# Down products of two blocks at a time: their 64-row rests in the two halves of the array's rows, each in its own PSUM bank

## The chip, the cores and the metric

The kernel runs on one core of a Trainium2 chip. The metric is the device time in microseconds of one execution; three runs of the kernel before give 792.35, 794.47 and 799.27 us, with a median of 794.47.

## The reference, cut to what matters

The whole computes two residual layers on 8 x 512 tokens of width 256. The first layer is a LoRA projection and a fake-quantised gated FFN. The second is the one the change touches: a per-language adapter with a norm, a router that takes the best two of nine experts for each token, and a gated FFN of inner width 704 in each expert.

```python
def _L1_ffn_ref(x, Wr, Wg, Wu, Wd):
    logits = jnp.einsum('bsh,he->bse', x, Wr)
    probs = jax.nn.softmax(logits, axis=-1)
    topk_w, topk_idx = jax.lax.top_k(probs, TOP_K)
    topk_w = topk_w / jnp.sum(topk_w, axis=-1, keepdims=True)
...
    gate = jax.nn.silu(jnp.einsum('th,ehi->tei', xf, Wg))
    hidden = gate * jnp.einsum('th,ehi->tei', xf, Wu)
    out = jnp.einsum('tei,eih,te->th', hidden, Wd, cw)
```

All of the second FFN is computed in f32. The inner width is 704 = 5 x 128 + 64: five full chunks of 128 rows and a rest of 64.

## The kernel before, in words

**Stages.** The first layer works with activations laid out with the width over the partitions: `lora_in` and `lora_out` (L258, L273) do the LoRA products in pairs of batches, a pair in the two halves of the array (64 columns each in L262, 64 rows each in L278, where each half writes its own PSUM bank); `gate_chunk` and `last_chunk` the quantised gate and up products. Then a software pipeline over 8 batches (the loop at L907) runs `down_and_add` (L469, bf16, five 128-row products and one 64-row product L477 for each bank), the adapter (L484, L512), transposes (L497, L557), the router (`choose`, L569) and `hand_out` (L603), which scatters each token's row to the list of each of its two experts in DRAM.

**Blocks.** The lists are worked off in blocks of 128 rows, each with one expert's weights; 72 blocks are planned for and 67 are used in the shown inputs. One block is: `fetch_rows`, `fetch_gate_up` and `fetch_down` (L792 to L817) by transfers of SyncE's queue; `turn` (L819), two transposes of the rows and a copy by ScalarE; `gate_up` (L828), 11 chunks of 128 columns by 2 products of 128 rows into three PSUM banks, then silu by ScalarE and the multiplication by VectorE into `hid` (128 x 6 x 128); `down` (L859), six products of `hid` against the down weights into one bank; then VectorE multiplies with the token's weight into `y` (L866) and GpSimd starts an indirect transfer that adds the 128 rows into the output (L867).

**The rest of 64 rows.** The last chunk of the inner width has 64 rows. The down weights hold these 64 rows twice, once in each half of the partitions of chunk 5. `hid[64:128, 5]` gets the rest (L848), and `hid[0:64, 5]` is set to zero once for each of the three `hid` buffers (L929 to L931), so that the sixth product can be a full one of 128 rows (L864).

**Order and buffers.** TensorE's and SyncE's orders are written by hand (`manual_schedule`, L900); those of the other engines are left to a scheduler. For block i TensorE does `gate_up(i)`, `turn(i + 1)`, then `down(i - 1)` (`first_half`, L886, and `second_half`, L893). Ten blocks are woven into the batch loop (`SLOTS`, L905); blocks 10 to 63 follow in the loop at L958, and the rest under a branch for each (L966), which ends with the last `down`. PSUM's eight banks are taken in turn (L447): three for a `gate_up`, one for a `turn`, one for a `down`. There are three buffers each of gate and up weights, down weights, `hid`, `g`, `y` and the token weights, and eight of rows. `ask(rows, gu, dn)` (L879) requests transfers up to the given block: gate and up weights of block i + 3 behind `gate_up(i)`, down weights of block i + 2 behind `down(i - 1)`. A block's weights are transferred only if its expert is not that of the block three before it. Before block 16 SyncE also writes the pad rows of the lists (`write_pads`, L758).

Of the kernel before, what the change touches and what calls it, by code (L numbers as in the profile page):

```python
# [28 lines left out]
ALU = mybir.AluOpType  # L29
AX = mybir.AxisListType  # L30

P = 128
# [6 lines left out]
def adaln_ffn_kernel(  # L39
# [21 lines left out]
    nc = tc.nc  # L61
# [3 lines left out]
    NL1, D, A = W1.shape  # L65
# [7 lines left out]
    NM = (I + P - 1) // P  # L73
# [11 lines left out]
    def act_scale(top, sig, name):  # L85
# [26 lines left out]
    start = rt.tile([P, NJ, E], F32, name="start")  # L112
    nc.gpsimd.iota(
        start, pattern=[[0, NJ], [CAP, E]], base=0, channel_multiplier=0, allow_small_or_imprecise_dtypes=True
# [6 lines left out]
    full = NM - 1  # L121
    last = rows[-1]
# [319 lines left out]
    def in_turn(name, of):  # L442

        turn_of[name] = turn_of.get(name, -1) + 1
        return of[turn_of[name] % len(of)]

    def bank(name):  # L447
        return in_turn("bank", banks_sb)
# [11 lines left out]
    def quantise(b):  # L460
        batches[b]["hq"] = hq = hq_sb[b % 2]
        batches[b]["x"] = x_sb[:, b]
        h = h_full(b // 2)[:, :, b % 2]
        for m0, m1 in ((0, 1), (1, 3), (3, 5)) if b == 0 else ((0, 3), (3, 5)):
            rounded(hq[:, m0:m1], h[:, m0:m1], rh)()
        if b % 2 == 0:
            rounded(hl_sb[b // 2 % 2], h_last(b // 2), rh)()
# [12 lines left out]
    def adapter_in(b):  # L480
        st = batches[b]
        ph = bank("ph")
        for c in range(KC):
            nc.tensor.matmul(  # L484
                ph[:A], lhsT=st["w1"][:, c], rhs=st["x"][:, c], start=c == 0, stop=c == KC - 1
            )
        st["ha"] = ha = ha_sb[b % 2]
        nc.scalar.activation(ha[:A], ph[:A], AF.Relu, bias=st["b1c"])
# [62 lines left out]
    def turn_z(b):  # L551
        st = batches[b]
        st["zT"] = zT = ad.tile([P, KC, S], F32, name="zT")
        for c in range(KC):
            pt = bank("pt3")
            for j in range(NJ):
                nc.tensor.transpose(  # L557
                    pt[:, j * P : (j + 1) * P], st["row"][:, j, c * P : (c + 1) * P], ident
                )
            nc.scalar.copy(zT[:, c], pt)  # L560
# [81 lines left out]
    SURE = 2 * T // P  # L642
    NW = 3
# [121 lines left out]
    AHEAD = 4  # L765
# [3 lines left out]
    def where_h_was(k, n):  # L769
        got = flat_h[k][:, at_[0] : at_[0] + n]  # L770
        at_[0] += n
        return got
# [9 lines left out]
    hid_sb = [where_h_was(1, NM * P).rearrange("p (m t) -> p m t", t=P) for _ in range(3)]  # L782
# [7 lines left out]
    steps = [dict() for _ in range(NBLK)]  # L790
# [28 lines left out]
    def turn(i):  # L819
        st = steps[i]  # L820
        xb = st["xb"]
        pt = bank("pt4")
        for c in range(KC):
            nc.tensor.transpose(pt[:, c * P : (c + 1) * P], xb[:, c * P : (c + 1) * P], ident)  # L824
        st["xbT"] = xbT = in_turn("xbT", xbT_sb)
        nc.scalar.copy(xbT.rearrange("p c t -> p (c t)"), pt[:, :D])  # L826

    def gate_up(i):  # L828
        st = steps[i]

        gu, xbT = st["gu"], st["xbT"]
        pa, pb, pd = bank("pga"), bank("pgb"), bank("pgc")
        spots = [(pa, m * P) for m in range(4)] + [(pb, m * P) for m in range(4)] + [(pd, 0), (pd, P), (pd, 2 * P)]
        st["hid"] = hid = in_turn("hid", hid_sb)
        g = in_turn("g", g_sb)
        for n, (bk, at) in enumerate(spots):
            for c in range(KC):
                nc.tensor.matmul(  # L838
                    bk[:, at : at + P], lhsT=gu[:, c, n * P : (n + 1) * P], rhs=xbT[:, c], start=c == 0, stop=c == KC - 1
                )  # L840
        nc.scalar.activation(g[:, :4].rearrange("p m t -> p (m t)"), pa, AF.Silu)  # L841
        nc.vector.tensor_tensor(  # L842
            hid[:, :4].rearrange("p m t -> p (m t)"), pb, g[:, :4].rearrange("p m t -> p (m t)"), ALU.mult
        )
        nc.scalar.activation(g[:, 4], pd[:, :P], AF.Silu)  # L845
        nc.vector.tensor_tensor(hid[:, 4], pd[:, P : 2 * P], g[:, 4], ALU.mult)  # L846
        nc.scalar.activation(g[last : 2 * last, 5], pd[:last, 2 * P : 3 * P], AF.Silu)  # L847
        nc.vector.tensor_tensor(  # L848
            hid[last : 2 * last, 5], pd[last : 2 * last, 2 * P : 3 * P], g[last : 2 * last, 5], ALU.mult
        )  # L850

        xb = st["xb"]
        m0, dw, wt = (in_turn(n, small_[n]) for n in ("m0", "dw", "wt"))
        nc.vector.tensor_scalar(m0, xb[:, D + 3 : D + 4], expert[:, i : i + 1], None, ALU.is_equal)
        nc.vector.tensor_tensor(dw, xb[:, D + 1 : D + 2], xb[:, D + 2 : D + 3], ALU.subtract)
        nc.vector.scalar_tensor_tensor(wt, dw, m0, xb[:, D + 2 : D + 3], ALU.mult, ALU.add)  # L856
        st["wt"] = wt

    def down(i):  # L859
        st = steps[i]  # L860
        hid, dn = st["hid"], st["dn"]
        po = bank("po")
        for m in range(NM):
            nc.tensor.matmul(po[:, :D], lhsT=hid[:, m], rhs=dn[:, m], start=m == 0, stop=m == NM - 1)  # L864
        y = in_turn("y", y_sb)
        nc.vector.tensor_scalar(y, po[:, :D], st["wt"], None, ALU.mult)  # L866
        nc.gpsimd.indirect_dma_start(  # L867
            out=out,
            out_offset=bass.IndirectOffsetOnAxis(ap=st["xb"][:, D : D + 1].bitcast(I32), axis=0),
            in_=y,  # L870
            in_offset=None,
            compute_op=ALU.add,
        )
# [5 lines left out]
    def ask(rows, gu, dn):  # L879

        for name, fetch, n in (("rows", fetch_rows, rows), ("gu", fetch_gate_up, gu), ("dn", fetch_down, dn)):
            while asked[name] < min(n, asked["planned"]):
                fetch(asked[name])
                asked[name] += 1

    def first_half(i):  # L886

        gate_up(i)
        ask(i + 1 + AHEAD, i + 1 + NW, i + NW - 1)
        if i + 1 < NBLK:  # L890
            turn(i + 1)

    def second_half(i):  # L893

        if i > 0:
            down(i - 1)
            ask(0, 0, i + NW)


    with tc.manual_schedule(engines={mybir.EngineType.SP, mybir.EngineType.PE}):  # L900
        quantise(0)
        quantise(1)
        done = 0

        SLOTS = {5: 1, 6: 2, 7: 2, 8: 2, 9: 1, 10: 2}  # L905
        PLANS = {4: 0, 8: 1, 10: 2}
        for i in range(B + 3):  # L907
            slots = SLOTS.get(i, 0)
            f = PLANS.get(i)
            if 1 <= i <= B:  # L910
                adapter_in(i - 1)
            if slots > 1:
                first_half(done)
            if 1 <= i <= B:
                turn_x(i - 1)
            if 3 <= i:
                hand_out(i - 3)
            if f is not None:
                plan_counts(f)
            if slots > 1:  # L920
                second_half(done)
                done += 1
            if i < B:
                down_and_add(i)
            if f is not None:
                plan_order(f)
            if i + 2 < B:
                quantise(i + 2)
            if i == 3:  # L929
                for hid in hid_sb:  # L930
                    nc.gpsimd.memset(hid[:last, full], 0.0)  # L931
            if 2 <= i < B + 2:
                turn_z(i - 2)
            if slots:
                if done == 0:
                    turn(0)
                first_half(done)
            if 1 <= i <= B:
                adapter_out_and_moments(i - 1)
            if f is not None:  # L940
                plan_blocks(f)
            if slots:
                second_half(done)
                done += 1
            if 1 <= i and i + 1 < B:
                fetch_adapter(i + 1)
            if 2 <= i < B + 2:
                choose(i - 2)
            if 1 <= i <= B:
                norm(i - 1)  # L950
            if f is not None and f < 2:
                asked["planned"] = ENDS[f + 1]
                if f == 0:
                    ask(0, 1, 1)
                    ask(1, 2, 2)
                ask(done + AHEAD, done + NW, done + NW - 1)
        pads_at = done + 6
        for i in range(done, SURE):  # L958
            if i == pads_at:
                write_pads()  # L960
                asked["planned"] = NBLK
            first_half(i)
            second_half(i)
    n_used = nc.values_load(used[0:1, 0:1], min_val=SURE - ENDS[2], max_val=NBLK - ENDS[2])

    def rest(i):  # L966
# [80 lines left out]
```

## Time and profile before

| What | us |
|---|---|
| Runs: lowest, median, highest | 792.35, 794.47, 799.27 |
| Profiled execution: its own time | 789.34 |
| Its span (first to last instruction) | 787.4 |
| TensorE busy, in matmuls | 707.1 (90%) |
| VectorE, ScalarE, GpSimd busy | 314.4, 222.2, 200.9 |
| First `gate_up` (block 0) starts | 201.9 |
| Block 10's `gate_up` starts | 335.9 |
| Last `down` ends on TensorE | 779.4 |

How to read it: the page divides the span into 40 slices of 19.7 us, with one digit for the busy tenths of each engine. A group of instructions is named by its line, engine, operation, and tiles written and read; "128*128 128x256 f32" of a matmul gives the rows and columns of the array that are used and the rows and columns of the moving operand. The end of a matmul in the records is modelled and overlaps the next one, so the distance between two starts tells the cost, not the recorded length. The profiled execution took 2 us more than its span.

### The profile page before, as it was taken

How to read it: one execution, taken by the hardware profiler on the slowest of the kernel's cores; microseconds unless marked ns; L12 is line 12 of the kernel's file. 1: busy time of each engine (PE TensorE's matmuls, PEld its weight loads, DVE VectorE, ACT ScalarE, POOL GpSimd, SP SyncE). 2: the span in 40 equal slices, each digit the busy share in tenths (PEclk: the TensorE clock that was granted, in tenths of full speed). 3: DMA queues.
4: the chain of work that ended last, by engine and by line, in shares of the span. 5: the costliest groups of instructions: out<-in, count | busy, mean ns of one | idle time of the engine just before them, and what ended most of it. 6: DMA issues, size and time to landing. Idle time of an engine off the chain costs nothing. (4 is left out here: it accounts for less than half of the span.)

```text
span 787.4 us, 13732 instructions
## 1 busy us (share of the span) xinstructions
PE 707.1 (90%) x4717; PEld 602.0 (76%) x4728; DVE 314.4 (40%) x1087; ACT 222.2 (28%) x439; POOL 200.9 (26%) x173
## 2 busy tenths in 40 slices
PE   7497596775799976999999999999999999999995
PEld 2233234552687866999999999999999999999995
DVE  3769864554356445422222222222222222222221
ACT  4588583342132132111111111211111111212110
POOL 1045500440323454241212122121212121221212
PEclk9799885666699988999999999999999999999999
DMA  9500011332846847632337331238942468315642
GB/s 344 163 1 2 0 34 48 101 102 81 328 136 168 301 129 266 204 82 35 78 82 236 105 81 29 42 102 275 333 107 40 144 218 266 79 28 156 180 116 30
DMA packets 44522, 103.38 MB, mean 131 GB/s; under 512 B 8216, under 2 KB 33824, under 8 KB 41120
## 3 DMA queue, kind: packets, MB, share of 16 engines
q1 hardware_dynamic: 31584, 85.13, 31.7%
q0 software_dynamic: 12720, 17.31, 12.2%
q8 instruction: 39, 0.64, 0.3%
q14 instruction: 35, 0.29, 0.1%
q10 hardware_dynamic: 144, 0.01, 0.0%
HBM read 176.86 MB, written 22.83 MB: 254 GB/s over the span
## 5 line engine op out<-in xcount | busy, mean ns | idle before, releaser
L838 PEld LDWEIGHTS bank<-upper__107,lower 128*128 128x128 f32 x2948 | 342.8, 194 | 7.1 <-issue 3.2
L838 PE MATMUL bank<-upper__107,lower 128*128 128x128 f32 x2948 | 344.3, 277 | 0.5 <-ACT upper__107 L826 0.5
L864 PE MATMUL bank<-upper__107 128*128 128x256 f32 x528 | 124.1, 385 | 0.0
L842 DVE TENSOR_TENSOR upper__107<-bank,upper__107 128x512 f32<-128x512 f32 x67 | 46.3, 691 | 178.6 <-PE bank L838 178.5
L864 PEld LDWEIGHTS bank<-upper__107 128*128 128x128 f32 x528 | 98.6, 193 | 12.2
L867 POOL DMA_INDIRECT out_dram<-upper__107,lower x35 | 54.8, 1565 | 189.7 <-DVE wt L856 133.8
L841 ACT ACTIVATE upper__107<-bank 128x512 f32<-128x512 f32 x67 | 39.9, 596 | 224.0 <-PE bank L838 224.0
L867 POOL DMA_INDIRECT out_dram<-upper__107 x32 | 50.0, 1564 | 180.7 <-DVE wt L856 154.1
L631 POOL DMA_INDIRECT lists<-row,sloti x64 | 63.0, 984 | 121.5 <-DMA lower<-lists 34.4
L866 DVE TENSOR_SCALAR upper__107<-bank,wt 128x256 f32<-128x256 f32 x67 | 32.4, 484 | 96.9 <-PE bank L864 96.7
L845 ACT ACTIVATE upper__107<-bank 128x128 f32<-128x128 f32 x67 | 18.6, 277 | 162.7 <-PE bank L838 162.7
L864 PE MATMUL bank<-lower,upper__107 128*128 128x256 f32 x276 | 63.5, 380 | 0.4 <-issue 0.4
L864 PEld LDWEIGHTS bank<-lower,upper__107 128*128 128x128 f32 x276 | 50.7, 190 | 6.8 <-issue 0.8
L846 DVE TENSOR_TENSOR upper__107<-bank,upper__107 128x128 f32<-128x128 f32 x67 | 19.5, 291 | 59.2 <-ACT upper__107 L845 59.2
L557 PE MATMUL bank<-ident,row 128*128 128x128 f32 x64 | 13.0, 370 | 21.5 <-DVE row L549 18.4
L848 DVE TENSOR_TENSOR upper__107<-bank,upper__107 64x128 f32<-64x128 f32 x67 | 19.7, 294 | 20.9 <-ACT upper__107 L847 20.3
L557 PEld LDWEIGHTS bank<-ident,row 128*128 128x128 f32 x64 | 10.4, 192 | 22.9 <-issue 18.6
L826 ACT COPY upper__107<-bank 128x256 f32<-128x256 f32 x68 | 25.3, 372 | 9.0 <-PE bank L824 8.8
L375 ACT ACTIVATE g<-pg,swg 128x1024 f32<-128x1024 f32 (+1 forms) x24 | 24.8, 1049 | 9.8 <-PE pg L363 6.6
L379 POOL TENSOR_TENSOR lower<-u,g 128x1024 f32<-128x1024 f32 x6 | 14.1, 2356 | 47.8 <-ACT u L378 47.8
L363 PE MATMUL pg<-yq,wgT 128*128 128x512 bf16 x79 | 22.6, 405 | 4.0 <-DVE yq L163 2.2
L476 PE MATMUL bank<-yq,wdT 128*128 128x512 bf16 x73 | 21.4, 409 | 3.2 <-DVE yq L163 2.5
(203 smaller groups left out, 663.2 us busy)
## 6 DMA issues: line engine op xcount, KB each, us to landing
lower<-in_L_ffn_W_dram SPq DMA_DIRECT2D x70, 1408.0 KB
upper__107<-in_L_ffn_W_dram SPq DMA_DIRECT2D x46, 768.0 KB
lower<-in_L_ffn_W_dram SPq DMA_DIRECT2D x23, 768.0 KB
lower<-lists SPq DMA_DIRECT2D x36, 130.0 KB
upper__107<-lists SPq DMA_DIRECT2D x35, 130.0 KB
x_sb<-in_x_dram SPq DMA_DIRECT2D x8, 512.0 KB
out_dram<-xtok SPq DMA_DIRECT2D x8, 512.0 KB
lists<-pad SPq DMA_DIRECT2D x10, 130.0 KB
```

The costliest lines, as they stand in the source:

```text
L363: nc.tensor.matmul(p[:, z * S : (z + 1) * S], lhsT=w[:, c, ms], rhs=yq[:, 2 * k + z, c], start=c == 0, stop=c == KC - 1,)
L375: nc.scalar.activation(g, pg[:, :n], AF.Silu, scale=swg[:, m : m + 1])
L476: nc.tensor.matmul(pd, lhsT=wdT[:, m, cs], rhs=hq[:, m], start=m == 0, stop=False)
L557: nc.tensor.transpose(pt[:, j * P : (j + 1) * P], st["row"][:, j, c * P : (c + 1) * P], ident)
L631: nc.gpsimd.indirect_dma_start(out=own_rows[(b * NJ + j) * 2 + k], out_offset=bass.IndirectOffsetOnAxis(ap=sloti[:, j, k : k + 1], axis=0) ...
L826: nc.scalar.copy(xbT.rearrange("p c t -> p (c t)"), pt[:, :D])
L838: nc.tensor.matmul(bk[:, at : at + P], lhsT=gu[:, c, n * P : (n + 1) * P], rhs=xbT[:, c], start=c == 0, stop=c == KC - 1)
L841: nc.scalar.activation(g[:, :4].rearrange("p m t -> p (m t)"), pa, AF.Silu)
L842: nc.vector.tensor_tensor(hid[:, :4].rearrange("p m t -> p (m t)"), pb, g[:, :4].rearrange("p m t -> p (m t)"), ALU.mult)
L864: nc.tensor.matmul(po[:, :D], lhsT=hid[:, m], rhs=dn[:, m], start=m == 0, stop=m == NM - 1)
L866: nc.vector.tensor_scalar(y, po[:, :D], st["wt"], None, ALU.mult)
L867: nc.gpsimd.indirect_dma_start(out=out, out_offset=bass.IndirectOffsetOnAxis(ap=st["xb"][:, D : D + 1].bitcast(I32), axis=0), in_=y, in_of ...
```

## The change

From block 10 on, blocks go by twos: `gate_up(i)`, `turn(i + 1)`, `gate_up(i + 1)`, `turn(i + 2)`, then the downs of blocks i - 1 and i together: five 128-row products of the one into its bank, five of the other into its bank, then the two 64-row rests behind each other. A block of odd number keeps its rest in partitions 0 to 63 of `hid`'s chunk 5, one of even number in 64 to 127 (`half`), so the two rests of a pair lie in different halves of the array's rows. The zeroing of the unused half is gone. The blocks woven into the batch loop, and those under the branches, still do one down at a time, its last product now over 64 rows. Down weights of two blocks are requested behind each pair.

```diff
+    def half(i):
+        return slice(0, last) if i % 2 else slice(last, 2 * last)
...
-            hid[last : 2 * last, 5], pd[last : 2 * last, 2 * P : 3 * P], g[last : 2 * last, 5], ALU.mult
+            hid[half(i), full], pd[last : 2 * last, 2 * P : 3 * P], g[last : 2 * last, 5], ALU.mult
...
-    def down(i):
+    def down(*blocks):
+
+        for i in blocks:
+            st = steps[i]
+            st["po"] = po = bank("po")
+            for m in range(full):
+                nc.tensor.matmul(po[:, :D], lhsT=st["hid"][:, m], rhs=st["dn"][:, m], start=m == 0, stop=False)
+        for i in blocks:
+            st = steps[i]
+            hs = half(i)
+            nc.tensor.matmul(st["po"][:, :D], lhsT=st["hid"][hs, full], rhs=st["dn"][hs, full], start=False, stop=True)
+        for i in blocks:
+            weigh_and_add(i)
+
+    def weigh_and_add(i):
         st = steps[i]
-        hid, dn = st["hid"], st["dn"]
-        po = bank("po")
-        for m in range(NM):
-            nc.tensor.matmul(po[:, :D], lhsT=hid[:, m], rhs=dn[:, m], start=m == 0, stop=m == NM - 1)
+        po = st["po"]
         y = in_turn("y", y_sb)
         nc.vector.tensor_scalar(y, po[:, :D], st["wt"], None, ALU.mult)
         nc.gpsimd.indirect_dma_start(
...
-    def first_half(i):
+    def first_half(i, downs_left=1):
 
         gate_up(i)
-        ask(i + 1 + AHEAD, i + 1 + NW, i + NW - 1)
+        ask(i + 1 + AHEAD, i + 1 + NW, i + NW - downs_left)
...
-            if i == 3:
-                for hid in hid_sb:
-                    nc.gpsimd.memset(hid[:last, full], 0.0)
...
-        for i in range(done, SURE):
+        assert (SURE - done) % 2 == 0 and pads_at % 2 == done % 2
+        for i in range(done, SURE, 2):
             if i == pads_at:
                 write_pads()
                 asked["planned"] = NBLK
             first_half(i)
-            second_half(i)
+            first_half(i + 1, 2)
+            down(i - 1, i)
+            ask(0, 0, i + 1 + NW)
```

## The prediction, made before the changed kernel ran

> **What bounds the kernel now.** I read the page first (busy shares and slices), then who waited for whom on TensorE over the block loop, then TensorE's timeline in the loop and in the early stages where the array already works on parts of its rows or columns.
>
> ```profile
> PE 707.1 (90%) x4717; PEld 602.0 (76%) x4728; DVE 314.4 (40%) x1087; ACT 222.2 (28%) x439; POOL 200.9 (26%) x173
> PE   7497596775799976999999999999999999999995
> PEclk9799885666699988999999999999999999999999
> L838 PE MATMUL bank<-upper__107,lower 128*128 128x128 f32 x2948 | 344.3, 277 | 0.5 <-ACT upper__107 L826 0.5
> L864 PE MATMUL bank<-upper__107 128*128 128x256 f32 x528 | 124.1, 385 | 0.0
> ```
> TensorE is at 9 in every slice from 335 us on, at a granted clock of 9 and more. 2948 is 67 x 44: a block's 22 gate and up products (11 chunks by 2) each leave two records, two passes of an f32 product; the down products too (528 + 276 = 67 x 12, for 6).
>
> The waits of TensorE between 330 and 780 us have one row in all:
> ```profile
> PE bank L864 <- issue: 0.4, 1, 0.4
> ```
> So from 330 us to the end the time is the sum of TensorE's passes. One block in its timeline (start, length, line):
> ```profile
> 335.86 5.07 PE L838 MATMUL bank<-upper__107,lower 128*128 128x128 f32 x44
> 340.77 0.38 PE L824 MATMUL bank<-ident,lower 128*128 128x128 f32 x2
> 340.99 2.76 PE L864 MATMUL bank<-lower,upper__107 128*128 128x256 f32 x12
> 343.58 5.07 PE L838 MATMUL bank<-upper__107,lower 128*128 128x128 f32 x44
> ```
> From start to start: 44 passes in 4.91 us, 12 down passes in 2.59 us (0.216 us each), a block in 7.72 us. The 379 ns of a record overlap the next; the pace is what costs.
>
> [...] The LoRA stage at the start has the very form of the change, 64-row f32 products in both row halves into two banks (L278, four products of 512 columns a time):
> ```profile
> 14.00 1.99 PE L278 MATMUL py<-t,small_sb 64*128 64x512 f32 x8
> 15.92 1.94 PE L262 MATMUL pr<-x_sb,small_sb 128*64 128x512 f32 x8
> 17.79 1.99 PE L278 MATMUL py<-t,small_sb 64*128 64x512 f32 x8
> ```
> Eight passes of 512 columns at the loop's pace are 8 x 0.432 = 3.46 us one after another; the eight took 1.92 us from the first to the next line's first. The single records start in twos, 5 to 7 ns apart. So the halves do run together, also in f32: 4 x 0.432 = 1.73, and 0.19 us is left over per visit. That rest is the change of mode: in the single records the first L278 starts 521 ns after the last L262 where 429 is the pace (0.092, the drain), and the next 534 ns later (0.105, the load of 128 columns). Two other places agree:
> ```profile
> 227.10 1.25 PE L476 MATMUL bank<-yq,wdT 128*128 128x512 bf16 x5
> 228.29 0.39 PE L477 MATMUL bank<-yq,wdT 64*128 64x512 bf16 x1
> 228.61 1.09 PE L557 MATMUL bank<-ident,row 128*128 128x128 f32 x8
> ```
> ```profile
> 240.77 1.93 PE L484 MATMUL bank<-x_sb,w 128*64 128x512 f32 x4
> 242.63 5.18 PE L838 MATMUL bank<-upper__107,lower 128*128 128x128 f32 x44
> 247.64 0.38 PE L824 MATMUL bank<-ident,upper__107 128*128 128x128 f32 x2
> ```
> L477 is a 64-row product behind 128-row ones in one accumulation, as the change makes it. Five L476 take 1.19 us to L477's start instead of 5 x 0.216 = 1.08, and L477 takes 0.32 instead of 0.216: about 0.10 for each of the two drains (bf16 weights, 10 ns of load). L838 behind a 64-column mode takes 5.01 us for its 44 passes instead of 4.91: another 0.10[...]. So one change of mode into f32 products costs about 0.093 drain + 0.105 load = 0.20 us.
>
> **The change part by part.** The program order shows the TensorE rows: two gate_ups, then ten 128-row down products, then the two 64-row ones, 27 times (blocks 9 to 62); blocks 0 to 8 and 63 to 66 keep one down each, now ended by one 64-row product.
>
> *Pairs.* Removed: two sixth products run one after another, 4 passes x 0.216 = 0.864. Added: drain and load 0.093 + 0.105, two overlapped passes 2 x 0.216 = 0.432 and 7 ns of stagger, drain and load of the next gate_up 0.093 + 0.102: 0.832. Gain 0.03 us a pair, 27 x 0.03 = -0.9 us. Bounds: the two mode changes measured between 0.17 and 0.21 each, so 0.01 to 0.09 a pair, -0.3 to -2.4.
>
> *Single downs.* A 64-row product takes as long as a 128-row one (L477 beside L476), so these only pay: 0.39 us where a 128-row f32 product follows, 0.30 where bf16 follows (L476), 0.20 where the next product (9 rows, L719) changed the mode before as well. In the tail, d63 and d64 pay 0.39 each on the full path, d65 only its entry 0.20; d66's scatter waits for d65's at 780.7, with its own y ready at 780.4, so its 0.2 is covered: +1.0 us. Early: d0 0.30, d1 0.39, d2 0.30, d3 0.39, d4 0.35 (it runs at half clock), d5 0.39, d6 0.39, d7 0.20, d8 0.39: 3.1 us. The first four, 1.4 us, stand ahead of a wait of TensorE of 4.85 us (L700 at 280.5 us for VectorE), whose chain goes over scatters that only partly start from TensorE: I count half, 0.7. After it the chain goes through TensorE at each step (the waits of 2.3 and 4.7 us at 299 and 302 us begin at its L569), so d4 to d8, 1.7 us, count but for 0.2 at a wait of 0.35 us: early +2.2, bounds +1.2 and +3.1.
>
> *Moved work.* A down of the first block of a pair comes one gate_up later, so y, its multiplication (484 ns) and its scatter (1.56 us on GpSimd, landing some 4 us later) come two at a time each 15.4 us: VectorE is busy 29% of the loop and GpSimd 20%, cover enough. In VectorE's order both y stand behind the second block's hid, which the next pair needs 10 us later: nothing. The 8 banks turn 10 times a pair, and each bank comes back over 5 us after its reader could start: nothing. The three hid buffers are all in use at a pair, but block i+2 writes behind the pair on TensorE anyway. SyncE asks the down weights of i+2 and i+3 together after the pair; for i+2 the time from request to use falls from 20.5 us (three blocks less a down) to 12.4 (two gate_ups 10.26, five products 2.16). In the trace the packets of such a load end 4.7 to 5.6 us after the request, with six full blocks in a row between 527 and 577 us: 7 us of cover. The requests behind those two in SyncE's order are for gate and up weights of blocks two pairs ahead. The nine pad writes (383 to 392 us) stay ahead of block 16; behind them the request for block 19 comes 5 us before use instead of 8, and no weight packets move there (none between 331 and 411 us). The three memsets left out ended at 123 us, GpSimd then waited 18 us for VectorE: nothing.
>
> *Sum.* -0.9 + 1.0 + 2.2 = +2.3 us on the profiled execution's 789.34 (span 787.4): 791.6. The shown runs have a median of 794.47, 5.1 above it, so 796.8 is my figure for a median.
>
> **The rivals.** (1) The mode change is cheap for f32 here: weights are loaded ahead, only drains are paid. Then a pair gains 0.864 - 0.432 - 0.19 = 0.24, -6.5, singles pay about half, +1.6: 789.6. If even the drain vanished, 27 x 0.43 = -11.6: 783. For it: in L278 loads for the second passes do go ahead within a mode. Against: the 0.10 at L838 and L477, every time. (2) It ends slower: the halves don't overlap, because the two accumulate behind 128-row products of their own banks and follow each other; decided by whether the second product starts 7 ns or 0.43 us after the first. Then a pair loses 0.40, +10.8, singles +3.2: 808.5. Against: L278 starts in twos with two banks. (3) Late weights: if a down load took over 12.4 us from request to landing, TensorE would stand in about 13 pairs with a fresh load; 1 us each gives 810, with 7 us of measured cover against it. (4) The switch is paid, but the early waits hide all: +0.5, 795.
>
> **How the numbers follow.** My case 0.80 (with (4) in its range), its own range 793 to 802: +0.5 to +3.9 and the spread of the shown runs, -2 to +5. Rival (1) 0.08 with drains alone and 0.03 without, (2) 0.05, (3) 0.04. The likeliest is 796.8; 788.5 to 804 takes in the cheap switch and leaves out the free one and both slow ones. One per cent (7.9 us) is about what can be told from no change. Over 1% faster: the free switch and some scatter, 0.06. Over 1% slower: (2), (3), scatter, 0.12. Within: 0.82.
>
> **What would show it.** In the changed profile's loop: the ten down passes of two blocks 20 x 0.216 = 4.3 us, then 64-row passes starting 7 ns apart, the first of them 0.31 after the last 128-row one; from the first 64-row start to the next gate_up 0.63 us; that gate_up's 44 passes 5.01 us; a pair in 15.41 us against 15.45. Passes 0.216 apart in the halves would prove (2), 0.22 ahead of the halves (1), a wait of TensorE for a transfer (3). What would make me wrong: a shift of the stages before 330 us by more than 3 us.

## The result, and the profile after

The changed kernel takes 816.94 us (median of 6 runs, 815.01 to 819.06) beside 794.05 us for the kernel before on the same chip: a ratio of 1.0275, 95% interval 1.0247 to 1.0304. It is slower by 19.6 to 24.1 us, where I had forecast +2.3 us and a range that ended at 804. The profiled execution took 819.02 us with a span of 817.2. That span is 29.8 us longer than the one before, more than the 22.9 us between the medians: the profile before (789.34) lies below all six runs of its kernel here, the profile after at the top of its own. The ratios and intervals of this document are taken over executions at the chip's usual speed (one slow execution of experiment 1 is left out), and are not the quotients of the medians that stand beside them.

On the page, TensorE is busier in microseconds and less busy as a share:
```profile
PE 719.7 (88%) x4717; PEld 588.3 (72%) x4728; DVE 308.1 (38%) x1087; ACT 221.8 (27%) x439; POOL 201.3 (25%) x170
L841 PE MATMUL bank<-upper__107,lower 128*128 128x128 f32 x2948 | 351.9, 279 | 16.6 <-ACT upper__107 L826 14.7
```
The second line is the gate and up products. They had stood idle for 0.5 us in all; now for 16.6 us, 14.7 of it waiting for ScalarE's copy at L826, which moves the transposed rows of `turn` from PSUM to `xbT`. The waits of TensorE from 345 to 800 us (total, times, longest) say how often:
```profile
PE bank L841 <- ACT upper__107 L826: 14.2, 27, 0.8
PE bank L841 <- issue: 1.7, 3, 1.1
```
Twenty-seven waits: one for each pair. One pair in TensorE's timeline (start, length, line), with the start of the next:
```profile
360.53 5.18 PE L841 MATMUL bank<-upper__107,lower 128*128 128x128 f32 x44
365.55 0.38 PE L824 MATMUL bank<-ident,upper__107 128*128 128x128 f32 x2
366.44 5.18 PE L841 MATMUL bank<-upper__107,lower 128*128 128x128 f32 x44 [0.52 <-ACT upper__107 L826]
371.46 0.38 PE L824 MATMUL bank<-ident,upper__107 128*128 128x128 f32 x2
371.68 2.32 PE L868 MATMUL bank<-upper__107 128*128 128x256 f32 x10
373.84 2.32 PE L868 MATMUL bank<-lower,upper__107 128*128 128x256 f32 x10
376.09 0.48 PE L872 MATMUL bank<-upper__107 64*128 64x256 f32 x1
376.10 0.48 PE L872 MATMUL bank<-lower,upper__107 64*128 64x256 f32 x1
...
376.72 5.18 PE L841 MATMUL bank<-upper__107,lower 128*128 128x128 f32 x44
```
The two rows of L872 are the first passes of the rests (their second passes, 0.32 us later, are left out): they start 6 ns apart in the trace, which the view rounds to 0.01 us, so the halves run together, 0.31 us behind the last full pass (373.84 + 9 x 0.216 = 375.78), and the next `gate_up` starts 0.63 us after them. All as forecast. The second and third rows are not: from the transposes of the second block to its `gate_up` 0.89 us pass, where two transposes followed by a down take 0.22. The other engines' rows between the two, and the restart:
```profile
365.81 0.28 ACT L848 ACTIVATE upper__107<-bank 128x128 f32<-128x128 f32 x1 [2.53 <-PE bank L841]
366.02 0.37 ACT L826 COPY upper__107<-bank 128x256 f32<-128x256 f32 x1
366.44 0.52 PEld L841 LDWEIGHTS bank<-upper__107,lower 128*128 128x128 f32 x4 [0.75 <-ACT upper__107 L826]
366.44 0.60 PE L841 MATMUL bank<-upper__107,lower 128*128 128x128 f32 x3 [0.52 <-ACT upper__107 L826]
```
ScalarE's copy starts at 366.02, behind the transposes, and takes 0.37 us; the products that read `xbT` start at 366.44, behind it. The weights come late too: the third row (PEld) shows the first load starting with the first product, not ahead of it. That `gate_up` needs 371.46 - 366.44 = 5.02 us for its passes instead of 4.91. So a pair pays 0.67 (0.89 - 0.22) and 0.11, and gets 0.03 back: 16.19 us from start to start, against 2 x 7.72.

In the profile before the same chain can be read, with a down in between that hides it. ScalarE's copy and the next `gate_up` there, between 340 and 344.5 us:
```profile
341.03 0.28 ACT L845 ACTIVATE upper__107<-bank 128x128 f32<-128x128 f32 x1 [2.53 <-PE bank L838]
341.52 0.37 ACT L826 COPY upper__107<-bank 128x256 f32<-128x256 f32 x1 [0.21 <-ACT upper__107 L845]
343.58 1.17 PE L838 MATMUL bank<-upper__107,lower 128*128 128x128 f32 x9
```
The transposes had started at 340.77 and the copy ended at 341.89, 1.12 us later; the down took TensorE from 340.99 to 343.58. Ahead of the second `gate_up` of each pair the change takes that cover away.

**Where the difference lies.** From the starts of the `gate_up` of single blocks in the timelines, in us. From block 12 to block 60 TensorE does nothing but blocks (48 of them, 24 pairs). The kernels of the experiments are in the table for what follows; of before there are three profiles, of after two (experiment 8).

| Kernel | start of block 10 | block 10 to 12 | 12 to 60 | 60 to the end |
|---|---|---|---|---|
| before, three times | 335.9, 332.7, 330.6 | 15.44 each | 370.64 each | 65.4, 65.4, 65.3 |
| after, twice | 341.5, 334.5 | 19.06, 16.47 | 388.60 each | 68.0, 68.0 |
| 1, transposes ahead of the downs | 338.7 | 17.21 | 369.84 | 66.1 |
| 2, pairs, rests over 128 rows | 335.9 | 18.79 | 389.40 | 66.9 |
| 3, old order, every rest alone | 346.9 | 18.58 | 389.44 | 68.1 |
| 4, a down behind each `gate_up`, rests by pairs | 335.6 | 17.44 | 369.84 | 66.4 |
| 5, the same, single blocks over 128 rows | 341.0 | 18.12 | 369.84 | 65.4 |
| 6, rests by fours | 337.0 | 19.45 | 364.95 | 69.0 |
| 7, rests by fours up to block 58 | 334.1 | 22.68 | 364.96 | 65.5 |

From block 12 to 60 the granted clock of TensorE is 1.00 in each of these twelve profiles, so the clock has no part in the difference there. From block 12 on the profiles of a kernel agree to 0.1 us: after loses 17.96 us in 24 pairs, 0.748 a pair. The first pair of the loop adds 1.0 (16.47 - 15.44) and the last column 2.6, of which two pairs are 1.5 and the single downs 1.1. That makes 21.6 of the medians' 22.9 us. The two columns ahead of block 12 are no measure of a few us from one profile: the same kernel differs by 5 to 7 us in the first and by 2.6 in the second.

### The profile page after: what moved, and what is told of

Read it like the earlier page. It is cut to its first block, busy times and chain, and to the rows that moved or that the text cites. A ratio compares the mean times of both kernels' runs of the same rounds, so it can differ in the third digit from the quotient of the medians.

```text
span 817.2 us, 13784 instructions
## 1 busy us (share of the span) xinstructions
PE 719.7 (88%) x4717; PEld 588.3 (72%) x4728; DVE 308.1 (38%) x1087; ACT 221.8 (27%) x439; POOL 201.3 (25%) x170
## 5 line engine op out<-in xcount | busy, mean ns | idle before, releaser
L841 PE MATMUL bank<-upper__107,lower 128*128 128x128 f32 x2948 | 351.9, 279 | 16.6 <-ACT upper__107 L826 14.7
L841 PEld LDWEIGHTS bank<-upper__107,lower 128*128 128x128 f32 x2948 | 339.3, 194 | 37.7 <-ACT upper__107 L826 21.6
L868 PE MATMUL bank<-upper__107 128*128 128x256 f32 x440 | 103.4, 386 | 0.0
L868 PEld LDWEIGHTS bank<-upper__107 128*128 128x128 f32 x440 | 83.0, 193 | 10.8
L880 DVE TENSOR_SCALAR upper__107<-bank,wt 128x256 f32<-128x256 f32 x67 | 29.9, 480 | 123.9 <-PE bank L872 113.6
L868 PE MATMUL bank<-lower,upper__107 128*128 128x256 f32 x230 | 53.6, 380 | 0.2 <-issue 0.2
L868 PEld LDWEIGHTS bank<-lower,upper__107 128*128 128x128 f32 x230 | 42.7, 190 | 5.8 <-issue 0.6
L826 ACT COPY upper__107<-bank 128x256 f32<-128x256 f32 x68 | 25.3, 371 | 10.5 <-PE bank L824 9.3
L851 DVE TENSOR_TENSOR upper__107<-bank,upper__107 64x128 f32<-64x128 f32 x67 | 19.7, 294 | 21.6 <-ACT upper__107 L850 20.8
L872 PE MATMUL bank<-upper__107 64*128 64x256 f32 x88 | 24.9, 434 | 0.0
```

The costliest lines, as they stand in the source:

```text
L841: nc.tensor.matmul(bk[:, at : at + P], lhsT=gu[:, c, n * P : (n + 1) * P], rhs=xbT[:, c], start=c == 0, stop=c == KC - 1)
L868: nc.tensor.matmul(po[:, :D], lhsT=st["hid"][:, m], rhs=st["dn"][:, m], start=m == 0, stop=False)
L872: nc.tensor.matmul(st["po"][:, :D], lhsT=st["hid"][hs, full], rhs=st["dn"][hs, full], start=False, stop=True)
```

## The experiments

My theory A: the loss is the copy's lost cover, and the change of mode (TensorE going from products over 128 rows to products over 64, and back) costs what I had said. Rival B: the mode changes cost far more than the 0.39 us there and back (the loads of the 64-row weights are late, and the idle time is only put down to the copy). Except where it is said, each edit is against the changed kernel; none leaves out a part of the computation.

**1. The transposes of the next pair ahead of the downs.** The two transposes of a pair's blocks go behind the previous pair's second `gate_up`, so that the downs hide both copies; the rests stay as in the changed kernel.
```diff
...
-            first_half(i)
+            if i == done:
+                turn(i + 1)
+            first_half(i, 1, False)
             first_half(i + 1, 2)
+            if i + 3 < SURE:
+                turn(i + 3)
             down(i - 1, i)
```


> The changed kernel with both transposes of a pair's next blocks moved behind the second gate_up, ahead of the downs, so that the copy of the transposed rows by ScalarE has the downs as cover again. Theory A (the time went into TensorE's wait for that copy, 0.52 us idle, 0.15 of latency and 0.10 of weights that cannot be loaded ahead in each of 27 pairs): about 20 us less than the changed kernel, 796 us, a ratio of 1.003 to the kernel before, and a pair in 15.4 us. Theory B (the time went into the changes of the tiling mode, or into waits for the later down weights): unchanged at 816 us.

Measured: 795.64 us beside 792.24, ratio 1.0023 (1.0000 to 1.0046). TensorE's timeline has the second `gate_up` of a pair joined to the first:
```profile
494.58 10.09 PE L841 MATMUL bank<-upper__107,lower 128*128 128x128 f32 x88
504.51 0.60 PE L824 MATMUL bank<-ident,lower 128*128 128x128 f32 x4
504.94 2.32 PE L868 MATMUL bank<-upper__107 128*128 128x256 f32 x10
```
No wait of TensorE is left from 345 to 775 us. A pair takes 15.41 us, 0.033 less than before (0.80 / 24): the figure that the prediction had for a pair without any new wait. The loss is gone with the mode changes all in place; A holds and B falls.

**2. Pairs without a change of mode.** The changed kernel's order, but the sixth products run over 128 rows, with the unused half set to zero as before.
```diff
-            hid[half(i), full], pd[...], g[last : 2 * last, 5], ALU.mult
+            hid[last : 2 * last, full], pd[...], g[last : 2 * last, 5], ALU.mult
...
-            nc.tensor.matmul(st["po"][:, :D], lhsT=st["hid"][hs, full], rhs=st["dn"][hs, full], start=False, stop=True)
+            nc.tensor.matmul(st["po"][:, :D], lhsT=st["hid"][:, full], rhs=st["dn"][:, full], start=False, stop=True)
...
```


> The order by pairs alone: all six down products over 128 rows as in the kernel before, with the zeroed halves, no mode changed. Theory A: the wait for the copy is there all the same, 27 x 0.75 = 20 us more than before, 814 us, ratio 1.026. Theory B: without mode changes the time is that of the kernel before, 794 us; if late down weights were the cause, 814 us too, but with waits of TensorE for a transfer in the profile.

Measured: 815.73 us, ratio 1.0296 (1.0234 to 1.0358). With no 64-row product in the blocks the loss is still there, 0.78 us a pair (18.76 / 24), and the wait too:
```profile
505.58 0.38 PE L824 MATMUL bank<-ident,upper__107 128*128 128x128 f32 x2
506.48 5.18 PE L841 MATMUL bank<-upper__107,lower 128*128 128x128 f32 x44 [0.52 <-ACT upper__107 L826]
```
The order alone makes the loss. The changed kernel loses (389.40 - 388.60) / 24 = 0.033 us less a pair: what the halves gain, a second time.

**3. The mode change alone.** The kernel before (the edit is against it) with its order, one down behind each `gate_up`, but every sixth product over 64 rows without a partner; the zeroing of the unused half is gone.
```diff
+            ks = slice(0, P) if m < full else slice(last, P)
-            nc.tensor.matmul(po[:, :D], lhsT=hid[:, m], rhs=dn[:, m], start=m == 0, stop=m == NM - 1)
+            nc.tensor.matmul(po[:, :D], lhsT=hid[ks, m], rhs=dn[ks, m], start=m == 0, stop=m == NM - 1)
...
```


> The kernel before with its order, but the sixth down product over its 64 rows alone, so that each of the 67 blocks goes into the 64-row mode and back with no partner. It measures the price of two mode changes by itself. Theory A, with the prices of the prediction: a block of the loop takes 7.72 + 0.39 = 8.11 us, in all 54 x 0.39 = 21 and some 3 us at both ends, 818 us, ratio 1.030. Theory B: if mode changes took the time of the changed kernel (27 pairs, 20 us more with 0.43 saved in each), one block would cost 1.2 us more, 874 us.

Measured: 814.90 us, ratio 1.0265 (1.0223 to 1.0306). A block takes 8.11 us:
```profile
500.49 2.95 PE L865 MATMUL bank<-lower,upper__107 128*128 128x256 f32 x12
503.37 5.18 PE L838 MATMUL bank<-upper__107,lower 128*128 128x128 f32 x44
508.38 0.38 PE L824 MATMUL bank<-ident,upper__107 128*128 128x128 f32 x2
```
The twelve passes take 2.88 us instead of 2.59, the `gate_up` behind them 5.01 instead of 4.91; over 48 blocks 18.80 / 48 = 0.392 each. So 0.39 us for a change of mode there and back is right to the hundredth in the loop. That its total is close to that of experiment 2 is chance: the one is 0.39 for each block, the other 0.78 for each two.

**4. The cover given back, the pairs kept.** Five products of a down behind each `gate_up`, as before, and the two rests together behind every second.
```diff
...
             first_half(i)
+            down_full(i - 1)
             first_half(i + 1, 2)
-            down(i - 1, i)
+            down_full(i)
+            down_rests(i - 1, i)
```


> The order of the kernel before for gate_up, turn and the five 128-row down products of each block, only the two 64-row rests together behind every second block. The copy has 2.2 us of down products as cover. Theory A: 796 us, ratio 1.003, a pair in 15.4 us, as with the transposes moved. Theory B: 816 us.

Measured: 794.24 us, ratio 1.0030 (1.0011 to 1.0048). No wait is left from 345 to 775 us; a down again stands behind the transposes, and the rests behind two of them:
```profile
496.94 2.32 PE L870 MATMUL bank<-upper__107 128*128 128x256 f32 x10
499.10 5.07 PE L841 MATMUL bank<-upper__107,lower 128*128 128x128 f32 x44
504.01 0.38 PE L824 MATMUL bank<-ident,lower 128*128 128x128 f32 x2
504.23 2.32 PE L870 MATMUL bank<-lower,upper__107 128*128 128x256 f32 x10
506.48 0.48 PE L876 MATMUL bank<-upper__107 64*128 64x256 f32 x1
```
A pair takes 15.41 us, as in experiment 1. With the cover back the total is where the prediction's sum had put it: +2.3 us on 794.47 is a ratio of 1.0029. What that match is worth is said below, under the sum.

**5. No single block over 64 rows.** Experiment 4, but blocks 0 to 8 and 63 to 66 keep the sixth product over 128 rows, with the unused half set to zero again.
```diff
+    PAIRED = range(9, SURE - 1)
...
+            hs = half(i) if i in PAIRED else slice(0, P)
...
```


> As the kernel with the downs between, but the blocks that have no partner (0 to 8 and 63 to 66) keep their sixth product over 128 rows with a zeroed half, so that only pairs change the mode. By the measured prices: a pair still gains 0.03 us, 27 pairs 0.9 us; the 3 us of mode changes of single blocks are gone. 0.1% less than the kernel before, ratio 0.999, which 5 rounds may not tell from 1. If single blocks' mode changes were hidden by waits before block 10: ratio 1.001 to 1.003, as with the downs between.

Measured: 796.29 us beside 794.09, ratio 1.0008 (0.9983 to 1.0032). The stretch from block 60 to the end is 65.4 us again, as before, where experiment 4 has 66.4: the tail's single downs cost 1.0. The effect of the early ones can't be told: the intervals of the two experiments overlap. By pairs alone the idea is worth 0.8 us in 24 pairs, too little to show.

**6. Rests by fours.** One change of mode there and back for four blocks (11 to 62). The edit is against the kernel before and keeps its order, with the rests of four blocks behind the fourth's five products. That needs four PSUM banks held (4 to 7; `gate_up` and `turn` take 0 to 3), buffers for the rests, more of `y` and the token weights, and a ScalarE copy of each block's 64 x 256 rest weights, because `dn` is overwritten before. The other blocks keep 128 rows.
```diff
+    QUADS = range(11, SURE - 1)
...
+    def down_rests(blocks):
+        for i in blocks:
+            at, k, hs = rest_at(i)
+            nc.tensor.matmul(steps[i]["po"][:, :D], lhsT=rest_sb[at][hs], rhs=rest_dn[k][hs], start=False, stop=True)
...
+                down_full(j)
+                if (j - QUADS.start) % QUAD == QUAD - 1:
+                    down_rests(range(j - QUAD + 1, j + 1))
```


> The rests of four blocks at a time (blocks 11 to 62), two and two side by side, behind the fourth block's five 128-row products: one change of mode there and back for four blocks. Rests and their weights lie in buffers of their own (ScalarE copies 64 x 256 weights for each block), four PSUM banks are held for the four sums, six y buffers, rows are asked for three blocks ahead. If a mode change is a fixed price of 0.2 us whatever is done in the mode: four blocks save 1.73 - 0.39 - 0.86 - 0.01 = 0.46 us, 13 times 6.0 us, ratio 0.992, faster than both kernels. If the price rises with each product in the mode (weights of every second product not loaded ahead, 0.1 each): 0.3 us and ratio 0.996. If four scatters in a row or the held banks make new waits, these stand in the profile as waits of TensorE, and the ratio is above 1.

Measured: 792.57 us, ratio 0.9974 (0.9951 to 0.9997). From block 12 to 60, twelve whole fours, 370.64 - 364.95 = 5.69 us are saved, 0.474 a four, beside 8 x 0.216 less 4 x 0.216 less 0.39 = 0.47. But from block 60 to the end 3.6 us come back. GpSimd's rows at the end, where each is the issue of one block's scatter into the output:
```profile
752.23 1.56 POOL L906 DMA_INDIRECT out_dram<-upper__107,lower  x1 [15.08 <-DVE upper__107 L905]
756.74 1.56 POOL L906 DMA_INDIRECT out_dram<-upper__107  x1 [2.96 <-DVE upper__107 L856]
...
780.21 1.56 POOL L906 DMA_INDIRECT out_dram<-upper__107,lower  x1 [2.90 <-DVE y L905]
784.75 1.56 POOL L906 DMA_INDIRECT out_dram<-y,lower  x1 [2.97 <-DMA out_dram<-upper__107,lower]
```
All eight of them follow each other at 4.5 to 5.3 us. The profile names the landing of the one ahead as releaser in two of the eight rows, the last among them; that it holds back the others too is read from their even steps. Four that become ready at once at 752 us push the last to 784.75; before, with a block each 7.7 us, it started at 781.50 (block 60 starts at 721.4 us here and 721.9 there).

**7. Fours that end earlier.** Against experiment 6: the fours stop at block 58, so that the queue of scatters can empty.
```diff
-    QUADS = range(11, SURE - 1)
+    QUADS = range(11, SURE - 5)
```


> The run of fours with its rests together, but the fours end four blocks earlier (blocks 11 to 58; blocks 59 to 66 alone, with the sixth product over 128 rows). If the stage of the fours is worth 0.515 us a four and the 4 us that the last stage grew by came from the last four's scatters standing one behind another, then 12 fours give -6.2 us, the stage after the last block is back at about 19.1 us, and the ratio is 0.991 to 0.994. If the longer end is not due to the scatters (the four held banks and buffers, say), it stays at about 23 us and the ratio is 0.997 to 0.999.

Measured: 787.81 us (6 runs) beside 791.97, ratio 0.9941 (0.9923 to 0.9960): faster than the kernel before by 3.2 to 6.1 us, and so than both. The stretch from block 60 to the end is 65.5 us, as before, so the longer end came with the last fours, as the row of scatters had it. The last two scatters:
```profile
776.83 1.56 POOL L906 DMA_INDIRECT out_dram<-upper__107,lower  x1 [6.16 <-DVE upper__107 L905]
781.42 1.56 POOL L906 DMA_INDIRECT out_dram<-y,lower  x1 [3.03 <-DMA out_dram<-upper__107,lower]
```
The expectation's 0.515 us a four was read over blocks 12 to 62, a stretch that cuts the last four before its rests. Whole fours give 0.474, and 12 x 0.474 = 5.7 us is 0.9928, inside the interval.

**8. The two kernels again.** One more profile of the changed kernel and two of the one before, without an edit, for the stages ahead of block 12. Those of before:

> The kernel before once more, for a second profile of its early stages. If its first profile was a short one there, block 10 starts later than 335.9 us, or the stretch from block 10 to block 12 takes 17 to 18.5 us with idle time of issue in its first products, as in each changed kernel so far, instead of 15.44. If the stretch is 15.4 us again, the 2 us and more that the other kernels take there belong to what they changed. Blocks 12 to 60 stay at 370.6 us.

> The kernel before a third time, with the same two outcomes as its second profile. The spread of the three starts of block 10 says how far single profiles can be compared before it.

That of after:

> The changed kernel a second time. If the spread before block 10 is that of single executions, block 10 starts elsewhere than at 341.5 us, by some us either way; from block 12 to 60 it takes 388.6 us again, since 24 pairs lose 0.748 us each.

Measured: 786.16, 783.96 and 809.39 us, one run each, on a chip where a further run of before took 787.99. From block 12 to 60 both kernels repeat to the hundredth, 370.64 and 388.60. Block 10 starts at 332.7 and 330.6 us in before, at 334.5 in after. TensorE's waits in after from 325 to 775 us are now one row, word for word the first of the two that the first profile had (14.2 us, 27 times). The idle time of "issue" in the first profile is gone, and the 27 waits are the same. So that idle time does not come with every execution of the changed kernel; why it comes in some of them stays open. Before has none of it between blocks 10 and 12 in any of its three profiles, with 15.44 us each time, and seven experiments all have 1.8 us or more over what their order explains there, so a cause in the changed code can't be excluded for those. It isn't one thing either: in experiments 3, 6 and 7 the stretch has a mean granted clock of 0.87, 0.91 and 0.85, in all the other profiles 1.00, and experiment 3 has no idle time of "issue" in it.

## Why the prediction was wrong

**What failed.** It is the step "Moved work": "so y, its multiplication (484 ns) and its scatter [...] come two at a time", with the answer "nothing" for `y` and for the banks, and no cost for `hid` and for the down weights. I asked of the moved down only who reads its result and when its buffers come free. I did not ask what it had hidden where it stood. In the order of before it fills TensorE while `turn(i + 1)` comes to its end and ScalarE copies (1.12 us from the start of the transposes to the end of the copy); within a pair `gate_up(i + 1)` follows its transposes directly. The term left out is 0.67 us of waiting and 0.11 us for first weights that are not loaded ahead there, 0.78 a pair (experiment 2 measures it alone); 27 x 0.78 = 21.1 us. Experiments 1 and 4 give the cover back in two ways, and the loss goes both times. The profile before had the numbers for it: transposes at 340.77, end of the copy at 341.89, and a down of 2.59 us between.

**Pair gain, 0.03 us.** Right: 0.033 in experiments 1, 4 and 5, and between the changed kernel and experiment 2. The new mechanism does all that it was to do; it is worth next to nothing by itself, since the two changes of mode cost what the overlap saves.

**Single downs.** The price, 0.39 us, was right (experiment 3: 0.392). The tail was right too: 1.1 us in the changed kernel, 1.0 between experiments 4 and 5, against +1.0. The early +2.2 is neither shown nor refuted. What a ratio leaves for the stages ahead of block 10, once the losses from there on are taken off, is in experiment 3 0.0265 x 792.24 = 21.0, less 18.8, 2.7 and 0.8 for two more blocks: -1.3 us. In the same way it is 0.2 in the changed kernel (1.3 by the medians), 1.9 in experiment 1 and 2.2 in experiment 4, which all have these products, and 2.1 in experiment 2 and 1.5 in experiment 5, which have none of them. Each is uncertain by 1.5 to 5 us. The profiles differ by more in that stage from one execution to the next than the term is large.

**The rivals.** (1), the cheap mode change, and (2), halves that follow each other, are out: 0.39 there and back, 6 to 7 ns of stagger. (3), late down weights: no wait of TensorE for a transfer appears after 345 us, so the cover that I had counted there was enough. (4), the early waits hide all, is within what stays open; its sum is -0.9 + 1.0 = +0.1, not the +0.5 that the prediction has. The outcome came on the slower side through a mechanism that none of them named. The sign that I had set for being wrong, a shift ahead of 330 us, looked in the wrong place, where even one kernel's profiles differ by 5 us; the pair's period, 16.19 us against the forecast 15.41, was the one that told.

**The sum.** Experiment 4 is the change as I had costed it, and it gives the forecast's ratio, 1.0030 (1.0011 to 1.0048) against 1.0029. So close a match is partly luck: 2.2 of the 2.3 us are the early term, which stays open, and the interval reaches from 0.9 to 3.8 us. What is shown are the terms of the pair and of the tail. The sum was that of an order in which a down still follows each transpose, which is not the order in the diff.

## What to carry to other kernels

When work is moved on the engine that sets the time, cost the place that it leaves as well as the place that it goes to: list what ran on other engines meanwhile (here the end of the transposes, the copy and the first weight load, 0.9 us behind a 2.6 us down) and who starts right behind it now. Packing half-array products into one mode paid here only when more than two shared one change of mode: two just break even (0.03 us), four save 0.47. And look at the end of the program when results come in bunches: what a bunch feeds one at a time, as the scatters at 4.5 us each, hides in the middle and stands bare at the end.

## What was not expected of the hardware

A change of mode around f32 products has a steady price here: 0.392 us there and back in each of experiment 3's 48 blocks, 0.29 ahead of and within the 64-row product and 0.10 at the first `gate_up` behind it. In one block of experiment 3 the passes from the last full one on start 0.309, 0.320 and 0.306 us apart, where the pace is 0.216, and the next 0.214, where it is 0.111. The first profile of the changed kernel has the same four distances within 1 ns in each of its 27 pairs (the third from the later half). The second and the last, 0.104 and 0.103 too long, are what the prediction calls the load: in these 27 pairs the first weight load of a new mode starts 1 to 2 ns ahead of its product and the next load 0.108 to 0.109 us after it, where between two full down passes a load starts 0.21 us ahead of its product. The first and the third, 0.093 and 0.090 too long, are what it calls the drain. Of these the traces show the delay alone, not what TensorE does in it; the name is my reading. So the two parts are about as dear. The same 0.10 us falls due without any change of mode at the first product behind the copy, where the load starts 1 to 2 ns ahead of it too: 5.02 us for 44 passes against 4.91, and 5.01 in experiment 2 (506.48 to 511.49), where no mode changes.
